# A memset on GpSimd behind the last accumulating DMA of a gated cross-attention and mixture-of-experts kernel

## The chip, the core and the metric

The kernel runs on one core of a Trainium2 chip. The metric is the device time of one launch in microseconds (us). The core has five engines that matter here, each with an instruction queue of its own: TensorE (PE in the profile, its weight loads PEld), VectorE (DVE), ScalarE (ACT), GpSimd (POOL) and SyncE (SP). They are held in order against each other by semaphores. Work that an engine's sequencer does itself (waits, branches, drains, issuing of DMAs) is written with a q: POOLq, SPq.

## The reference

The input `x` is 8 x 256 tokens of width 256. The reference adds a gated cross-attention to it and then a gated mixture of experts:

```python
x = x + tanh(g_xattn[0]) * xattn(layernorm(x), ctx, w_q, w_kv, w_out, b_out)   # 16 heads of 64, 120 context rows
x = x + tanh(g_ffn[0])   * ffn(layernorm(x), W1, W2, Wr)

def ffn(x, W1, W2, Wr):                       # 8 experts of width 1024, the best 2 of each token
    probs = softmax(x @ Wr.T)
    vals, idx = top_k(probs, 2)
    gate = one_hot(idx) weighted by vals / vals.sum()
    h = silu(x @ W1[e].T);  y = h @ W2[e].T   # for each expert e
    return sum over e of gate[e] * y
```

All of it is in float32.

## The kernel before, in words

The kernel first runs the attention, eight batches one after the other. While it does so it normalizes the attention's result, picks two experts for each token and scatters every token's row into a list in HBM (`routed`), one list for each expert. The attention's result itself is stored to the output `out`, so that the mixture of experts only has to be added to it.

In the second part the lists are worked off in tiles of 128 rows. The first eight tiles have a fixed expert, then come tiles of which a table computed on the chip says which rows and which expert they are (`order`, with `("full", j)` for j from 8 to 30). Tiles of four quarter lists (`quad`) run between them. For each tile, `up` multiplies by the first weight matrix, `down` multiplies by the second, scales by the gate into `y`, and `add_up` adds the 128 rows of `y` to the rows of `out` that they belong to. This is an indirect DMA issued from GpSimd with `compute_op=ALU.add`. As the same token stands in two lists, the adding DMAs must not overlap. The kernel therefore chains them by hand: each one waits until the one before it has landed, which the list `last_add` carries.

The order on TensorE, VectorE, ScalarE and SyncE is the order of the program text (`manual_schedule`); GpSimd is not in that list, but in the last part of the program it has nothing to run except the chained adding DMAs. The last `close_tile()` of the program issues the last `down` and with it the last adding DMA. Behind it the program ends: leaving the `TileContext` (line 1321 of the profile) emits, on every engine, the closing DRAIN and a barrier over all engines, with SP waiting for the outstanding DMAs first.

Of the kernel before, what the change touches and what calls it, by code (L numbers as in the profile page):

```python
# [9 lines left out]
F32 = mybir.dt.float32  # L10
# [5 lines left out]
P = 128  # L16
# [32 lines left out]
def tile_gated_xattn_moe(  # L49
# [978 lines left out]
    def close_tile():  # L1028
        if state["pending"] is not None:
            down(*state["pending"])  # L1030
            state["pending"] = None
# [248 lines left out]
            load_expert(7)  # L1280
    close_tile()


# [41 lines left out]
```

## Time and profile before

| what | us |
|---|---|
| median of 3 runs | 540.91 |
| lowest and highest run | 540.51, 541.64 |
| the profiled execution, device time | 540.71 |
| the profiled execution, span of its instructions | 538.9 |
| TensorE busy in it | 525.8 (98%) |
| VectorE, ScalarE, GpSimd busy | 285.1, 219.8, 128.7 |
| last TensorE work ends about | 528.6 |
| last adding DMA is issued at | 530.5 |

The span runs from the program's first instruction to its last. The 1.8 us between span and device time lie outside of the program's own instructions. The profile's page gives for each engine its busy time, then the span in slices, the DMA queues, the chain of work that ended last, and the costliest groups of instructions by source line. Instructions of a sequencer do not count as busy time, so a stretch in which only sequencers work looks empty in the slices; the views by source line show them.

### The profile page before, as it was taken

What the parts mean: (1) busy time and instruction counts of PE and PEld (TensorE: products, weight loads), DVE (VectorE), ACT (ScalarE), POOL (GpSimd) and SP (SyncE); (2) the same over time, 40 slices, a digit from 0 to 9 for tenths busy, and PEclk for the clock granted to TensorE, in tenths of its full rate; (3) what the DMA queues carried; (4) which work ended last, traced back from release to release, by engine and by line L of the source; (5) the groups of instructions that cost most, each with busy time, mean ns of one, the idle gap of its engine ahead of it and who ended that gap; (6) DMA issues with size and microseconds to landing.
All of it is one profiled execution on the core that took longest, in us unless ns stands there. A gap on an engine that the chain in (4) does not pass through costs nothing. (4 is left out here: it accounts for less than half of the span.)

```text
span 538.9 us, 9932 instructions
## 1 busy us (share of the span) xinstructions
PE 525.8 (98%) x3698; PEld 444.8 (83%) x3698; DVE 285.1 (53%) x683; ACT 219.8 (41%) x700; POOL 128.7 (24%) x135
## 2 busy tenths in 40 slices
PE   8999999999999999999999999999999999999992
PEld 7788887878878788787889999998997878889991
DVE  3675656567765677645663447444453453543530
ACT  1666546464664645557530311011144635501110
POOL 2011100000332003310014473222322124343422
PEclk9999999999999999999999999999999999999997
DMA  8999980140521401111099932312221210321311
GB/s 299 337 309 298 309 246 21 51 144 2 177 79 47 171 1 40 42 52 31 1 316 328 308 90 63 50 30 44 38 43 21 41 34 7 51 46 12 50 22 19
DMA packets 46439, 57.53 MB, mean 107 GB/s; under 512 B 3184, under 2 KB 41456, under 8 KB 46384
## 3 DMA queue, kind: packets, MB, share of 16 engines
q1 hardware_dynamic: 39488, 47.35, 28.6%
q0 software_dynamic: 6480, 8.81, 9.2%
q8 instruction: 32, 0.52, 0.4%
q10 hardware_dynamic: 416, 0.66, 0.4%
q14 instruction: 23, 0.19, 0.1%
HBM read 28.67 MB, written 28.27 MB: 106 GB/s over the span
## 5 line engine op out<-in xcount | busy, mean ns | idle before, releaser
L574 ACT ACTIVATE pr<-psc,mx 128x120 f32<-128x120 f32 x256 | 88.4, 372 | 64.5 <-DVE mx L568 64.5
L874 PEld LDWEIGHTS ph_full<-xT_full,w 128*128 128x128 f32 x736 | 85.0, 192 | 6.5 <-issue 5.7
L874 PE MATMUL ph_full<-xT_full,w 128*128 128x128 f32 x736 | 86.8, 276 | 0.3 <-PEq L1194 0.3
L890 PE MATMUL py_full<-w,hT_full 128*128 128x256 f32 x368 | 83.1, 379 | 0.0
L890 PEld LDWEIGHTS py_full<-w,hT_full 128*128 128x128 f32 x368 | 68.2, 190 | 8.4
L882 ACT ACTIVATE hT_full<-ph_full 128x1024 f32<-128x1024 f32 x23 | 23.5, 1023 | 97.7 <-PE ph_full L874 97.7
L524 PE MATMUL pq<-xnT,w_sb 128*128 128x256 f32 x256 | 62.7, 388 | 0.4 <-DVE xnT L207 0.4
L915 POOL DMA_INDIRECT out_dram<-y_full,xt_full x23 | 39.0, 1697 | 99.8 <-DVE y_full L898 70.4
L618 PE MATMUL pw<-w_sb 128*128 128x256 f32 x256 | 58.5, 382 | 0.0
L574 ACT ACTIVATION_READ_ACCUMULATOR pr<-psc,mx 128x1 f32 x256 | 55.7, 218 | 0.0
L524 PEld LDWEIGHTS pq<-xnT,w_sb 128*128 128x128 f32 x256 | 46.6, 190 | 10.8 <-issue 3.1
L618 PEld LDWEIGHTS pw<-w_sb 128*128 128x128 f32 x256 | 47.7, 190 | 9.0 <-issue 2.5
L562 DVE TENSOR_REDUCE mx<-psc 128x8 f32<-128x960 f32 x32 | 37.0, 1156 | 31.1 <-PE psc L554 31.1
L365 POOL DMA_INDIRECT routed<-rows,slot x32 | 32.1, 1002 | 54.4 <-DVE slot L361 47.4
L594 ACT COPY w_sb<-tr 120x512 f32<-120x512 f32 x64 | 34.6, 597 | 20.1 <-PE tr L593 20.1
L583 DVE TENSOR_TENSOR pr<-pr,sm 128x960 f32<-128x960 f32 x32 | 37.1, 1158 | 1.1
L554 PE MATMUL psc<-kT,w_sb 64*128 64x120 f32 x512 | 37.2, 284 | 0.0
L898 DVE TENSOR_SCALAR y_full<-py_full,gate 128x256 f32<-128x256 f32 x23 | 11.1, 484 | 48.5 <-PE py_full L890 44.8
L962 ACT COPY part<-w_sb 128x1024 f32 x32 | 31.1, 1043 | 14.1 <-PE py_q L1001 13.5
L554 PEld LDWEIGHTS psc<-kT,w_sb 64*128 64x128 f32 x512 | 31.1, 187 | 6.4 <-issue 3.6
L593 PEld LDWEIGHTS tr<-ident,pr 128*120 128x120 f32 x256 | 29.5, 138 | 5.5 <-issue 2.5
L845 DVE COPY w<-w_sb 128x2048 f32 x23 | 28.8, 1251 | 9.5 <-issue 4.3
(177 smaller groups left out, 670.6 us busy)
## 6 DMA issues: line engine op xcount, KB each, us to landing
routed<-w_sb SPq DMA_DIRECT2D x8, 2120.0 KB, 21.4
w_sb<-in_w1T_dram SPq DMA_DIRECT2D x8, 1024.0 KB, 5.7
w_sb<-in_w2T_dram SPq DMA_DIRECT2D x8, 1024.0 KB, 9.9
xt_full<-routed SPq DMA_DIRECT2D x23, 132.5 KB, 2.1
out_dram<-x SPq DMA_DIRECT2D x8, 256.0 KB, 2.4
x<-in_x_dram SPq DMA_DIRECT2D x7, 256.0 KB, 2.8
w_sb<-in_w_kv_dram SPq DMA_DIRECT2D x3, 512.0 KB, 8.0
xt_first<-routed SPq DMA_DIRECT2D x8, 132.5 KB, 2.5
```

What stands on the lines that cost most here:

```text
L365: send = nc.gpsimd.indirect_dma_start(out=routed[:, :], out_offset=bass.IndirectOffsetOnAxis(ap=slot[:, i : i + 1], axis=0), in_=rows[h][: ...
L524: nc.tensor.matmul(pq[:, i, :], lhsT=wq_sb[:, c, ts(2 * h + i, P)], rhs=xnT[:, c, :], start=(c == 0), stop=(c == DC - 1),)
L554: nc.tensor.matmul(psc[:, j, ts(i, M)], lhsT=qT[ts(j, DH), 4 * o + i, ts(nb, P)], rhs=kT[ts(j, DH), 4 * o + i, :], start=True, stop=True,)
L562: nc.vector.tensor_reduce(mx.rearrange("p (j i) -> p j i", i=4), psc[:, :, : 4 * M].rearrange("p j (i m) -> p j i m", m=M), AX.X, ALU.max,)
L574: nc.scalar.activation(pr[:, h, :], psc[:, j, ts(i, M)], AF.Exp, bias=mx[:, h : h + 1], scale=QK_SCALE, accum_out=sm[:, h : h + 1],)
L583: nc.vector.tensor_tensor(pr, pr, sm.unsqueeze(2).to_broadcast([P, 8, M]), ALU.mult)
L594: nc.scalar.copy(pT_sb[:, ts(j, 4), ts(nb, P)], tr[:M, :, :])
L618: nc.tensor.matmul(pw[:, :D], lhsT=oT_sb[b % 2][:, ci, ts(k, P)], rhs=wo_sb[:, ci, :], start=(ci == 0), stop=(ci == IC - 1),)
L874: nc.tensor.matmul(ph[:, f, :], lhsT=w1[:, c, ts(f, P)], rhs=xT[:, c, :], start=(c == 0), stop=(c == DC - 1),)
L890: nc.tensor.matmul(py[:, :D], lhsT=hT[:, f, :], rhs=w2[:, f, :], start=(f == 0), stop=(f == FC - 1),)
L915: add = nc.gpsimd.indirect_dma_start(out=out[:, :], out_offset=bass.IndirectOffsetOnAxis(ap=slots[:, k : k + 1], axis=0), in_=y[own, :], i ...
L962: nc.scalar.copy(w[:, q, :].rearrange("p (a b) -> p a b", b=D if down else DFF // 2), slab[:, ts(h, FC // 2), :] if down else slab[:, :, t ...
```

## The change

Behind the last `close_tile()` a tile of 128 x 1 float32 is allocated in the pool `const`, GpSimd sets it to zero, and that memset is given a dependency, with a semaphore wait, on the last adding DMA: it runs once the DMA has landed. Nothing reads the tile. No other line changes.

```diff
     close_tile()
 
+    end = const.tile([P, 1], F32, name="end")
+    mark = nc.gpsimd.memset(end, 0.0)
+    tc.add_manual_dep(
+        mark.ins,
+        last_add[-1].ins.name,
+        mybir.DependencyInfo(
+            mybir.DependencyClass.Sync, mybir.DependencyReason.DATA
+        ),
+        reason="behind the last sum",
+    )
+
```

## The prediction

> **What bounds the kernel now.** I read the page first, then the chain of waits that ended last, then the end of the span in windows, and last every instruction of the source line at which the program closes (L1321) and of the line that issues the sums (L915).
>
> ```profile
> span 538.9 us, 9932 instructions
> PE 525.8 (98%) x3698; PEld 444.8 (83%) x3698; DVE 285.1 (53%) x683; ACT 219.8 (41%) x700; POOL 128.7 (24%) x135
> ```
>
> Up to the last matmul TensorE is the bound: 525.8 of 538.9 us. The change does not touch any of that. It stands behind the last sum, so the question is only what fills the ten microseconds after TensorE.
>
> Windows of the end (columns: stretch, its length, busy time and count of PE, PEld, DVE, ACT, POOL, granted TensorE clock, DMA share, GB/s):
>
> ```profile
> 527.00:532.10 5.10, 1.61 (x8) 1.07 (x6) 0.48 (x1) 0.00 (x0) 2.05 (x2) 1.00 0.24 26
> 532.10:534.40 2.30, 0.00 (x0) 0.00 (x0) 0.00 (x0) 0.00 (x0) 0.00 (x0) 0.69 0.49 57
> 534.40:538.90 4.50, 0.00 (x0) 0.00 (x0) 0.00 (x0) 0.00 (x0) 0.00 (x0) 0.50 0.00 0
> ```
>
> The last sum's packets move in the middle window. In the third, 4.5 us long, no engine is busy and no DMA moves. What stands there is seen at the closing line (columns: engine, operation, count, shortest/median/longest in ns, first and last start in us):
>
> ```profile
> L1321 SPq EVENT_SEMAPHORE  x14: 17/28/4511, 512.8 to 538.9; - x14
> L1321 POOLq EVENT_SEMAPHORE  x4: 17/17/17, 538.1 to 538.8; - x4
> L1321 POOLq DRAIN  x3: 46/113/7812, 530.3 to 538.6; - x3
> L1321 DVEq DRAIN  x2: 19/272/524, 528.7 to 538.4; - x2
> ```
>
> GpSimd's first closing DRAIN takes 7812 ns. The chain of waits has its start, the timeline the last sum that it was dispatched with, and the waits of SP's queue what it costs SP:
>
> ```profile
> 530.27 1.77 POOLq L1321
> ...
> 530.49 1.54 POOL L915 DMA_INDIRECT out_dram<-y_full,xt_full  x1 [2.99 <-issue]
> ...
> DMA to landing us min/median/max: 2.2/3.8/8.1
> ...
> SPq L1321 <- PEq L1321: 3.9, 2, 3.4
> ```
>
> The DRAIN thus runs from 530.27 to 538.08. GpSimd's record of the last sum ends at 530.49 + 1.54 = 532.04. The sum lands at about 530.5 + 3.8 = 534.31 (SP's own record of its wait for that semaphore ends at 534.34). SP is through its list of waits at 534.87 and stands in the barrier for 3.4 us until GpSimd comes. So the end is set by GpSimd's DRAIN, and it lasts 6.04 us past the end of the sum's record and 3.77 us past its landing. After it, barrier and clearing of semaphores take 538.91 - 538.08 = 0.83 us.
>
> **The change part by part.** *The tile* is 4 bytes a partition that nobody reads; no address or order that the trace shows depends on it: nothing, if no other tile moves. *Removed or moved*: nothing. Every sum, load and matmul stays where it is, and nothing is queued behind the memset on GpSimd except the closing DRAIN; who waits for that DRAIN is the barrier, that is, all engines.
>
> *The wait.* The memset can begin when the last sum has landed, 534.31, plus the release: the wait ahead of the last sum ended 0.03 us after its semaphore's last step. That gives 534.34. It is 2.3 us after GpSimd's record was empty; in the kernel before those 2.3 us lay under the DRAIN, so by itself the wait costs nothing if the DRAIN needs the landing anyway, and 2.3 us if it does not.
>
> *The memset.* The nearest rows are the memsets of the same form at the program's start:
>
> ```profile
> L1306 POOL MEMSET const-float32-0.0<- x1: 99/99/99, 0.3 to 0.3; 128x1 f32 x1
> L1306 POOLq DRAIN  x1: 171/171/171, 0.4 to 0.4; - x1
> ```
>
> 0.10 us, so it ends at 534.44. Bound above: between the end of the wait at 529.78 and the last sum's dispatch GpSimd's sequencer spent 0.49 us; with that the memset would end at 534.93. I take 534.44, since a memset needs no DMA to be prepared.
>
> *The DRAIN behind it* is the whole question: the trace has no DRAIN of GpSimd that comes after a landed sum and a memset. The bounds from the nearest rows are 0.17 us (the DRAIN behind the four memsets at the start, no DMA issued before it) and 7.81 us (the long one whole). Between them lie 3.77 us (its part past the landing) and 6.04 us (its part past the sum's record). The tail after it stays 0.83 us. From the span of 538.91:
> - 0.17 us: ends at 534.61, but SP arrives only at 534.87, so the span would be 534.87 + 0.83 = 535.70, that is 3.2 us less;
> - 3.77 us: 534.44 + 3.77 + 0.83 = 539.04, 0.1 us more;
> - 6.04 us: 534.44 + 6.04 + 0.83 = 541.31, 2.4 us more;
> - 7.81 us: 543.08, 4.2 us more.
>
> I take 6.04 us. The long DRAIN isn't explained by waiting alone: when the data has landed, SP is released within 0.03 us, and still 3.77 us follow in which nothing moves. Something is being worked off, and the earliest it can have started is when GpSimd had handed out the last sum, at 532.04. The other engines' first closing DRAINs end with their last instruction (VectorE: 528.65 + 0.48 against 528.66 + 0.52), so the stretch belongs to GpSimd and to what it has done since the start: 73 indirect DMAs (32 + 23 + 8 + 8 + 2). The same engine's DRAIN before the first of these took 0.17 us and the one right after the long one 0.11 us, so the work is there once, after DMAs, and is gone when it has been done. Over 73 DMAs 6.04 us would be 0.08 us each. A memset after the landing does none of that work; it only starts it at 534.44 in place of 532.04.
>
> A rule of the Trainium skill speaks for the change: the page "PSUM — Partial Sum Buffer", section "Engine vs sequencer instructions", says that a drain waits until the engine is fully idle. By it alone the DRAIN would end with the memset and the sum would be the first line of the list above. The trace does not agree: the engine's last record ends at 532.04 and the DRAIN at 538.08.
>
> Another speaks against it: "GPSIMD Engine Reference", section "2.1 Instruction dispatch", has a cost of about 6 us, with no instruction of its own in the profile, for the first call to code just loaded. If the stretch of 6.04 us were such a load it would be paid behind the memset as well, and the sum would be the third line. No run here shows a loading of GpSimd's code.
>
> **The rivals.** *Short DRAIN, faster (0.36).* The long DRAIN may be long because it was dispatched with a DMA in flight: an inspection that found the sum unfinished and looked again only microseconds later. For it: the DRAIN does outlast the landing by a round 3.8 us without visible work, and with the landing waited for by a semaphore there is nothing unfinished to find. Against it: nothing else on this engine reacts that slowly; its waits for sums end 0.03 us after the landing. The price is the first line: 540.91 - 3.2 = 537.7. It decides when the DRAIN behind the memset takes less than 2.5 us.
>
> *Work that starts at the landing, no difference (0.14).* If the stretch of 3.77 us begins with the landing whatever stands between, the memset only shifts it by its own 0.13 us: 541.0. For it: 16 DMA engines looked at in turn at a quarter microsecond each would make such a stretch. Against it: VectorE and ScalarE show no such closing work, and nothing in the trace ties the 3.77 us to the landing rather than to the issue.
>
> *Fixed length, slower still (0.05).* If the DRAIN costs 7.81 us from its dispatch, the time is 545.1. Against it: 1.77 us of the 7.81 are the wait for the sum's record, which was under way.
>
> *The wait isn't there* could be the case if the memset were placed earlier or its wait were dropped; then it ends by 532.2 and the DRAIN is as before: 540.9 to 541.1, within the second rival's chance.
>
> **How the numbers follow.** The forecast, work of 6.04 us that starts behind the memset, has 0.42; 0.03 more is for shorter forms of it, 1.1 to 2 us over the time before. Its sum is made against the profiled execution: 540.71 + 2.40 = 543.11. That execution lies 0.20 us below the median of the runs, so a median would be 543.3. The runs lie from 0.40 below to 0.73 above their median, and the memset may be later by 0.49 us: the forecast's own range is 542.7 to 544.1. The whole range has to reach the fast rival: 537.7 less 0.4 gives 537.3. Above, it ends at 544.1 and leaves out the fixed length. A measurement of this kernel tells about 0.2% from no change, 1.08 us: slower by more has 0.42 + 0.03 + 0.05 = 0.50, within it 0.14, faster by more 0.36.
>
> **What would show it right or wrong.** In the profile of the changed kernel the closing line's first GpSimd DRAIN tells all: its start near 534.4 with a length near 6 us is the forecast, a length under 1 us the fast rival, near 3.8 us the neutral one. The memset should begin 0.03 to 0.5 us after the last landing and take 0.1 us. SP's wait in the barrier, 3.4 us before, should grow to near 5.7 us; under the fast rival it all but goes. If the span before 530.5 differs by more than a microsecond, the tile has moved something and the reasoning is wrong from its start.

## The result and the profile after

| | before | after |
|---|---|---|
| median of 6 runs, us | 540.70 | 543.42 |
| lowest and highest run, us | 540.42, 541.64 | 542.87, 544.57 |
| the profiled execution: device time, span, us | 540.71, 538.9 | 544.57, 542.8 |

The ratio after to before is 1.005, with a 95% interval from 1.004 to 1.0061: the memset makes the kernel 2.7 us slower by the medians and 2.45 us slower from lowest run to lowest run. The profiled execution of the changed kernel is the highest of its six, so it has to be read with care: not all of its 3.9 us are the change's.

First the page's head, then the end in windows cut at the same events as before (columns: stretch, its length, busy time and count of PE, PEld, DVE, ACT, POOL, granted TensorE clock, DMA share, GB/s):

```profile
span 542.8 us, 9933 instructions
```

```profile
528.40:533.50 5.10, 1.64 (x8) 1.11 (x6) 0.48 (x1) 0.00 (x0) 2.08 (x2) 0.94 0.24 26
533.50:535.80 2.30, 0.00 (x0) 0.00 (x0) 0.00 (x0) 0.00 (x0) 0.03 (x1) 0.50 0.50 57
535.80:542.77 6.97, 0.00 (x0) 0.00 (x0) 0.00 (x0) 0.00 (x0) 0.07 (x1) 0.50 0.00 0
```

One instruction more, the memset. The first two windows are as before. The third, in which no DMA moves and no engine but GpSimd is busy for 0.07 us, has grown from 4.50 to 6.97 us. The closing line, now L1332, says what stands there (engine, operation, count, shortest/median/longest in ns, first and last start), and the memset's own line what released it:

```profile
L1332 SPq EVENT_SEMAPHORE  x14: 17/28/4478, 512.8 to 542.7; - x14
L1332 POOLq EVENT_SEMAPHORE  x4: 17/17/17, 542.0 to 542.7; - x4
L1332 POOLq DRAIN  x3: 46/112/6179, 535.8 to 542.5; - x3
L1332 DVEq DRAIN  x2: 19/270/522, 530.1 to 542.2; - x2
```

```profile
L1284 POOL MEMSET end<- x1: 100/100/100, 535.8 to 535.8; 128x1 f32 x1
...
  DMA out_dram<-y_full,xt_full: 2.3, 1
```

GpSimd's first closing DRAIN has become shorter, 6179 ns in place of 7812, and it starts 5.5 us later. The timeline puts the four events in their order:

```profile
530.08 0.48 DVE L898 TENSOR_SCALAR y_full<-py_full,gate 128x256 f32<-128x256 f32 x1 [2.97 <-PE py_full L890]
531.93 1.55 POOL L915 DMA_INDIRECT out_dram<-y_full,xt_full  x1 [3.00 <-issue]
535.77 0.10 POOL L1284 MEMSET end<- 128x1 f32 x1 [2.29 <-DMA out_dram<-y_full,xt_full]
```

The last sum lands at 535.72, the memset runs from 535.77 to 535.87, and the DRAIN ends at 541.93, 6.06 us after the memset. SP, which stood 3.4 us in the barrier, stands there for 5.9:

```profile
SPq L1332 <- PEq L1332: 6.4, 2, 5.9
```

Part of the profiled execution's extra time arose 520 us earlier. The last `y` is made at 530.08 in place of 528.65, 1.43 us later. The timelines show where: the first matmuls of L480 wait for their weights in this execution and did not in the one before (first line after, second before).

```profile
8.75 2.04 PE L480 MATMUL pk<-ctxT_sb,w_sb 128*128 128x120 f32 x16 [1.36 <-DMA w_sb<-in_w_kv_dram]
```

```profile
7.34 1.96 PE L480 MATMUL pk<-ctxT_sb,w_sb 128*128 128x120 f32 x16
```

The tile isn't needed for it: of three kernels below that have the same tile and memset, two start these matmuls at 7.14 and 7.21, and the third, at 8.29, waits for the same load. It is a load at the program's start that lands now earlier, now later. The change's own cost is therefore read from the start of the last `y` to the end of the span: 538.91 - 528.65 = 10.27 us before, 542.77 - 530.08 = 12.70 us after, that is 2.43 us more.

### The profile page after: what moved, and what is told of

Same layout as the page of the kernel before. It is cut to its first block, busy times and chain, and to the rows that moved or that the text cites. A ratio compares the mean times of both kernels' runs of the same rounds, so it can differ in the third digit from the quotient of the medians.

```text
span 542.8 us, 9933 instructions
## 1 busy us (share of the span) xinstructions
PE 525.9 (97%) x3698; PEld 444.9 (82%) x3698; DVE 285.3 (53%) x683; ACT 219.8 (40%) x700; POOL 128.2 (24%) x136
## 5 line engine op out<-in xcount | busy, mean ns | idle before, releaser
L915 POOL DMA_INDIRECT out_dram<-y_full,xt_full x23 | 40.2, 1748 | 101.0 <-DVE y_full L898 75.0
```

The lines of the kernel that those rows point to most:

```text
L915: add = nc.gpsimd.indirect_dma_start(out=out[:, :], out_offset=bass.IndirectOffsetOnAxis(ap=slots[:, k : k + 1], axis=0), in_=y[own, :], i ...
```

## The experiments

The open question after the result was what GpSimd's DRAIN does for 6 us. The theory: it works off something for each DMA that GpSimd has issued since its last DRAIN, 0.083 us each. The rivals: a fixed stretch of 6 us, paid once or at each DRAIN; a stretch tied to the landing; the memset or its wait itself.

**The memset without its dependency.** The edit against the changed kernel:

```diff
-    mark = nc.gpsimd.memset(end, 0.0)
-    tc.add_manual_dep(mark.ins, last_add[-1].ins.name, ...)
+    nc.gpsimd.memset(end, 0.0)
```

> The memset stays at the end, its wait for the last landing is gone. Theory W (the closing DRAIN of GpSimd works off something left by the indirect DMAs, some 6.0 us, and starts it when GpSimd has nothing else to do): the memset runs right behind the last sum's record, about 0.2 us, and the DRAIN lies where it lay in the kernel before, over the landing: 540.7 to 540.9 us, 2.7 us less than with the wait, DRAIN ending about 6.1 us after the sum's record. Rival M (the memset itself, another kind of instruction between the DMAs and the DRAIN, is what costs): 543.4 us, as with the wait.

Measured: 540.64 us against 540.81, ratio 1.0004 (0.9995 to 1.0013). But the memset went elsewhere, as its row shows:

```profile
L1284 POOL MEMSET end<- x1: 89/89/89, 5.2 to 5.2; 128x1 f32 x1
```

With nothing to hold it, it was scheduled to 5.2 us after the program's start. The run shows that tile and instruction cost nothing; of a memset behind the last sum it tells nothing. It is repeated properly as the next one.

**The memset behind the last sum, without waiting for its landing.** The dependency is kept for the order in the queue alone:

```diff
-            mybir.DependencyClass.Sync, mybir.DependencyReason.DATA
+            mybir.DependencyClass.NoSync, mybir.DependencyReason.SCHED_ONLY
```

> The memset stands behind the last sum in GpSimd's queue, but without a wait for its landing (the memset of the earlier try without the wait had moved to the program's first microseconds, so that it told nothing of a memset behind the DMAs). Theory W (0.083 us of work for each DMA since the last DRAIN, begun when GpSimd is free): memset and DRAIN begin at the end of the last sum's record, the DRAIN ends 6.1 to 6.2 us after it, 540.7 to 541.0 us. Rival M (a memset between the DMAs and the DRAIN costs by itself): 543.4 us. If the DRAIN is long only because a DMA is in flight when it begins, it stays as before: 540.8 us.

Measured: 541.25 us against 540.84, ratio 1.0002 (0.9985 to 1.0018). Timeline of the end and closing DRAINs:

```profile
531.43 1.54 POOL L915 DMA_INDIRECT out_dram<-y_full,xt_full  x1 [2.99 <-issue]
532.41 0.68 POOL L1284 MEMSET end<- 128x1 f32 x1
```

```profile
L1332 POOLq DRAIN  x3: 46/113/7912, 531.2 to 539.7; - x3
```

The memset's record starts before the sum's has ended (532.98) and ends 0.11 us after it, at 533.09. The DRAIN ends at 539.15, 6.06 us behind the memset, though the sum only lands at 535.17. From the last `y` to the end of the span there are 10.39 us, 0.12 more than before, about as much as the memset's end lies behind the sum's record. So neither the memset nor its place in the queue costs anything that the times of the runs show; the wait does, because it holds back the start of a stretch of 6.06 us which, with 73 DMAs, begins just as well while the sum is in flight.

**One DRAIN in an idle stretch in the middle.** The edit against the kernel before, in `add_up`, so that GpSimd drains while it waits for the next tile anyway:

```diff
             last_add.append(add)
+            if t == ("full", 15):
+                settled = nc.gpsimd.drain()
+                tc.add_manual_dep(settled.ins, add.ins.name, ...Sync, DATA...)
```

> The kernel before with one DRAIN of GpSimd more, behind the landing of the sum of full tile 15, at about 410 us; 50 of the 73 indirect DMAs come before it and 23 after it. GpSimd is idle there for 6 us. Theory W, with 6.04 / 73 = 0.083 us for each DMA since the last DRAIN: the new DRAIN takes 4.1 us, the closing one has 1.9 us of work and ends with the landing of the last sum, at about 534.4 in the clock of the profile before, so 3.2 us less: 537.5 us. Rival F (6 us once, whatever came before, such as the loading of code): the new DRAIN takes 6 us, the closing one none, 537.5 us as well, but the length of the new one tells them apart. Rival G (every DRAIN behind DMAs takes 6 us): 6 us at both places, 540.7 us or a little more. Rival L (a DRAIN needs 3.8 us from the last landing): the new one 3.8 us, the closing one unchanged, 540.7 us.

Measured: 537.82 us against 540.81, ratio 0.9946 (0.9932 to 0.996). The added DRAIN's line, the closing DRAINs and SP's wait in the barrier:

```profile
L939 POOLq DRAIN  x1: 4157/4157/4157, 409.5 to 409.5; - x1
```

```profile
L1331 POOLq DRAIN  x3: 46/112/4923, 529.9 to 535.4; - x3
```

```profile
SPq L1331 <- PEq L1331: 1.2, 2, 0.6
```

Behind 50 DMAs, all landed, the added DRAIN takes 4.16 us (4.1 expected), and the closing one ends 4.9 us after its start instead of 7.8. A stretch that is paid once would have gone to the added DRAIN whole; a fixed one at each DRAIN would show 6 us twice. Neither does. One thing missed: with 23 DMAs left, work of 1.9 us that starts at the sum's record (531.68) would have been over before the landing at 533.86, and the DRAIN ended at 534.84, 0.98 us behind it.

**That DRAIN and the memset of the change.** Here everything has landed when the closing DRAIN starts its work.

> The changed kernel (memset behind the landing) with one DRAIN more behind the landing of the sum of full tile 15, so that 23 DMAs are left for the closing DRAIN. Theory W: the closing DRAIN begins behind the memset, 0.13 us after the landing, and takes 23 x 0.083 = 1.9 us; the end is 2.9 us after the landing (1.9 + 0.13 + 0.83), where it was 6.06 + 0.13 + 0.83 = 7.0 us in the changed kernel: 539.3 us, 4.1 us less than the changed kernel and 1.0 to 1.5 us more than with the additional DRAIN alone (537.8). If the DRAIN's work were the same whatever is left: 543.4 us.

Measured: 539.15 us against 540.84, ratio 0.9966 (0.9955 to 0.9977).

```profile
534.52 0.10 POOL L1294 MEMSET end<- 128x1 f32 x1 [2.31 <-DMA out_dram<-y_full,xt_full]
```

```profile
L1342 POOLq DRAIN  x3: 46/113/2069, 534.5 to 537.1; - x3
```

The DRAIN ends at 536.575, 1.954 us behind the memset's end at 534.621. With 73 DMAs the same stretch behind the same memset takes 6.06 us; with 23 it takes 1.95. The memset's wait, its place and its landing are the same in both: the stretch goes by the DMAs.

**Two DRAINs, the second three tiles before the end** (behind `("full", 15)` and `("full", 28)`).

```diff
-            if t == ("full", 15):
+            if t in (("full", 15), ("full", 28)):
```

> The kernel before with two DRAINs of GpSimd more: behind the landing of the sum of full tile 15 and behind that of full tile 28, where 2.2 us lie before the next sum; 2 DMAs are left for the closing DRAIN. Theory W: the second DRAIN takes 21 x 0.083 = 1.75 us and delays nothing, the closing DRAIN ends about 0.1 us after the last landing; then SP's list of waits, 0.55 us after the landing, is last: about 0.4 us less than with one additional DRAIN, 537.4 us, which is the floor of this way. If the 0.98 us by which the closing DRAIN outlasted the landing there are a fixed cost: 537.8 us.

Measured: 537.79 us against 540.84, ratio 0.994 (0.9923 to 0.9957).

```profile
L939 POOLq DRAIN  x2: 1757/2957/4157, 410.3 to 524.0; - x2
```

```profile
L1331 POOLq DRAIN  x3: 46/113/4121, 531.0 to 536.0; - x3
L1331 SPq DRAIN  x3: 7/7/13, 535.4 to 535.7; - x3
```

The first again takes 4157 ns; the second, behind 21 more DMAs, 1757. Two are left for the closing one; it ends at 535.08, 0.12 us behind the landing (534.96), and now SP is last: it reaches its own DRAIN only at 535.4. So the second DRAIN gains little: from the last `y` to the span's end there are 7.08 us against 7.36 with one, and the medians, 537.79 and 537.82, don't tell the two kernels apart. The time expected, 537.4, was 0.4 us too low.

**A DRAIN early** (behind `("full", 9)`, 42 DMAs after the start, 31 left), to settle what happens while the last sum is in flight.

```diff
-            if t == ("full", 15):
+            if t == ("full", 9):
```

> The additional DRAIN of GpSimd stands behind the landing of the sum of full tile 9, at about 365 us: 42 DMAs before it, 31 left for the closing one. Theory W: the new DRAIN takes 42 x 0.083 + 0.02 = 3.5 us. With 23 left the closing DRAIN had ended 0.98 us after the landing, though 1.9 us of work from the end of the record would have been over before it. If half of the work has to wait for the landing of the sum in flight: with 31 left it ends 0.083 x 31 / 2 = 1.3 us after it. If it is a fixed delay: 0.98 us. If the work is done in one go from the record: 2.6 us after the record, 0.3 us after the landing. Time in all three 537.5 to 538.3 us.

Measured: 538.30 us against 540.79, a single run of each, so only the trace is read here.

```profile
L939 POOLq DRAIN  x1: 3500/3500/3500, 365.5 to 365.5; - x1
```

```profile
L1331 POOLq DRAIN  x3: 52/113/5245, 530.5 to 536.3; - x3
```

The added DRAIN takes the 3.5 us expected. The closing one ends at 535.74, 1.31 us behind the landing at 534.43. The stretch behind the landing is thus neither a constant (0.98) nor gone (0.1 to 0.3): with 2, 23 and 31 DMAs left it is 0.12, 0.98 and 1.31 us, in each case close to half of 0.083 us times the number.

**More DMAs: four kernels.** Each adds 32 DMAs from GpSimd that write a constant to a scratch tensor that nobody reads. Large ones have 128 rows of 512 bytes, small ones 16 rows of 128 bytes.

```diff
+    aside = tc.dram_tile([32 * P, P], F32, name="aside")
...
+        if b == 5 and k == 2:
+            for m in range(32):
+                nc.gpsimd.dma_start(aside[ds(m * P, 128), :128], ones[:128, :128])
```

The first two (large, and small with `16` and `:32`) had nothing to hold them in the middle.

> The kernel before with 32 more DMAs issued from GpSimd in the idle time of the sixth batch of the attention (from about 250 us on), each of 128 rows of 512 bytes from a constant tile into a scratch tensor that nobody reads. Theory W with 0.083 us for each DMA: the closing DRAIN has 105 DMAs to work off, 8.7 us from the end of the last sum's record: 2.65 us more than before, 543.4 us. Rivals F, G and L (a fixed length): 540.7 us, as long as the additional DMAs delay nothing.

> As with 32 more DMAs of 128 rows, but each of 16 rows of 128 bytes. If the work of the closing DRAIN is by the DMA: 543.4 us, as with the large ones. If it is by the row or the descriptor: an eighth of it, 0.3 us more than before, 541.0 us. Fixed length: 540.7 us.

Measured: 550.26 us (large) and 551.15 us (small) against 540.81, ratios 1.016 (1.014 to 1.018) and 1.0193 (1.0173 to 1.0213). Most of that isn't the DRAIN. The DMAs were scheduled to the program's start, among the first loads. Windows of the first 40 us, kernel before and kernel with the small ones:

```profile
0.00:40.00 40.00, 37.60 (x259) 31.27 (x260) 22.59 (x70) 19.88 (x80) 5.65 (x22) 1.00 1.02 315
```

```profile
0.00:40.00 40.00, 31.80 (x200) 26.16 (x202) 16.35 (x60) 15.63 (x61) 20.46 (x53) 0.91 1.02 303
```

TensorE does 200 matmuls there in place of 259. The times are no measure of the DRAIN, but its own length is:

```profile
L1326 POOLq DRAIN  x3: 46/113/8349, 540.8 to 549.7; - x3
```

```profile
L1326 POOLq DRAIN  x3: 46/112/10426, 537.9 to 548.9; - x3
```

With the small ones (second fence) it ends 8.66 us behind the last sum's record: 105 DMAs at 0.0825 us. With the large ones it ends only 6.58 us behind it, where 8.7 were expected.

The other two hold the 32 DMAs back to about 238 us, where the loads are through:

```diff
+        if b == 6 and k == 3:
+            for m in range(32):
+                extra = nc.gpsimd.dma_start(aside[ds(m * P, 16), :32], ones[:16, :32])
+                tc.add_manual_dep(extra.ins, sends[-1].ins.name, ...Sync, DATA...)
```

> The kernel before with 32 more small DMAs of GpSimd (16 rows of 128 bytes each), now held back until the first scatters of the second group of batches have landed, at about 235 us, since in the earlier try they had moved to the program's start and delayed its loads by some 8 us. Theory W: the closing DRAIN ends 105 x 0.083 = 8.7 us after the last sum's record, 2.6 us more than before: 543.4 us, if nothing on the way waits for the additional DMAs. Fixed length: 540.8 us.

> As with the 32 small DMAs held back to about 235 us, but each of 128 rows of 512 bytes. At the program's start such large ones had lengthened the closing DRAIN by only 0.5 us, where the small ones had lengthened it by 2.6. Theory W alone (0.083 us for each DMA since the last DRAIN): the closing DRAIN ends 8.7 us after the last sum's record. Theory W with a bound (what is left by DMAs has room for a limited number of rows, and the oldest is worked off when it is full): 6.0 to 7.0 us, whenever the large ones are issued. If at the start it was the place and not the size: 8.7 us.

Measured: small 543.90 us against 540.84, ratio 1.0056 (1.0034 to 1.0078); large 541.39 us against 540.79, a single run of each. The last sum and the closing DRAINs, small, then large:

```profile
531.03 1.54 POOL L917 DMA_INDIRECT out_dram<-y_full,xt_full  x1 [3.05 <-issue]
```

```profile
L1334 POOLq DRAIN  x3: 46/113/10426, 530.8 to 541.8; - x3
```

```profile
530.57 1.54 POOL L917 DMA_INDIRECT out_dram<-y_full,xt_full  x1 [2.94 <-issue]
```

```profile
L1334 POOLq DRAIN  x3: 46/113/8426, 530.4 to 539.3; - x3
```

The small ones, at a place where they delay nothing, add 2.6 us to the stretch, which ends 8.66 us behind the sum's record, and 3.06 us to the kernel's median (from the last `y` to the end of the span: 2.68 us). So a DMA of 16 short rows costs as much as one of the sums. The large ones add less: the DRAIN ends 6.66 us behind the record, and 6.58 where they came early. From the landing, though, the two agree to the nanosecond: the last sum lands at 534.433 and the DRAIN ends at 538.777, and with the early ones at 544.817 and 549.161, in both 4.344 us later. Half of 0.083 us times 105 is 4.36. Read this way, the half of the stretch that comes behind the landing is there in full, and only the half ahead of it is shorter: it is over by the landing, 2.2 to 2.3 us behind the record, where half of the 8.66 us would take 4.3. This is a reading of two traces; no DRAIN behind large DMAs was run that starts with everything landed. The 6.0 to 7.0 us expected of a bound on what is left for the DRAIN were met, but no run shows such a bound, and why the first half is shorter stays open.

## Why the prediction was right

Put together, the DRAINs that started with everything landed:

| DMAs since the last DRAIN | length, us | 0.083 x number + 0.02 |
|---|---|---|
| 21 (second of the two added) | 1.757 | 1.76 |
| 23 (added one and memset, closing) | 1.954 | 1.93 |
| 42 (added behind tile 9) | 3.500 | 3.51 |
| 50 (added behind tile 15) | 4.157 | 4.17 |
| 73 (the changed kernel, closing) | 6.061 | 6.08 |

The slope is (6.061 - 1.757) / 52 = 0.083 us for each DMA.

*The tile, nothing:* held; without its dependency the same memset changes nothing that can be measured.

*The memset, 0.03 to 0.5 us behind the landing and 0.10 us long:* it came 0.05 us behind it and took 0.10 us.

*The DRAIN behind it, 6.04 us, as work of 73 DMAs at 0.08 us each:* 6.06 us, and the number of DMAs as its cause is shown by taking them away (23, 21) and adding small ones (105). The time since the last DRAIN, which an added DRAIN shortens as well, isn't the cause: the 32 small DMAs lengthen the stretch from 6.04 to 8.66 us at the same distance from it. The reason given for choosing 6.04 us, that the stretch can have started no earlier than the sum's record, agrees with the memset without a wait: the same 6.06 us, but from 533.09.

*The sum, +2.40 us:* the part of the trace that the change touches grew by 2.43 us. The medians differ by 2.72, the lowest runs by 2.45.

*SP's wait, near 5.7 us:* 5.9.

*"If the span before 530.5 differs by more than a microsecond, the tile has moved something":* it differs by 1.43 us, and the conclusion drawn there was wrong. The shift comes from the wait for `w_kv` at 7.4 us. That test should have been written on the stretch from the last `y` to the end, since a single execution's start varies by more than the test allowed.

*The short DRAIN, the chief rival at 0.36,* is ruled out by the same row: no DMA was in flight when the DRAIN began, and it still took 6 us. Its price was right for a DRAIN that is short: with two added DRAINs there are 7.08 us from the last `y` to the end in place of 10.27, the 3.2 us less that the prediction gave for it. The Trainium skill's page "PSUM — Partial Sum Buffer", section "Engine vs sequencer instructions", has a drain wait until the engine is fully idle. The traces show that this isn't all on GpSimd: engine idle from 535.87, all DMAs landed, and the DRAIN ends at 541.93.

*The load of code, which would have given the same number:* "GPSIMD Engine Reference", section "2.1 Instruction dispatch", has about 6 us for the first call to code just loaded. That the trace showed 6 us as well was chance; DRAINs of 1.76, 3.50 and 4.16 us, two of them in one program, don't fit a load of fixed length.

*The fixed length from the dispatch (0.05)* would have shown 7.81 us again; the DRAIN's record is 6.18.

*The stretch tied to the landing (0.14)* has a true part that the prediction missed. With the 73 DMAs of the kernel before, the work is bound by its length from the sum's record, 6.04 us. With few left, the landing sets the end, plus about half of the work: 0.12, 0.98 and 1.31 us with 2, 23 and 31 DMAs, and 4.344 with 105 of which 32 are large, in each case 0.041 us for each DMA and some 0.04 us more. Read together: without the large DMAs, the DRAIN ends at the later of the two, the record's end plus 0.083 us per DMA, or the landing plus half of that. For the kernel before the second is 534.31 + 3.0 = 537.3, the first 538.1, and 538.08 was measured. With the large ones the second alone fits.

What the DRAIN does for each DMA, and why about half of it comes behind the last landing, no run here shows.

## What to carry to other kernels

When a program ends some microseconds after its last data has landed, look at the closing line by engine: a sequencer's DRAIN isn't counted as busy, and the windows show it only as emptiness. Here a DRAIN of GpSimd that begins with everything landed costs 0.083 us for every DMA that the engine issued since its last one, so where that work outlasts the landing, anything that makes it start later, even a memset of 0.1 us with a wait, moves the end by the whole delay. The opposite move pays: one DRAIN where GpSimd waits anyway made the kernel before 3 us faster (537.82 us, ratio 0.9946), and it is enough that most of the DMAs lie before it: a second one just ahead of the end brought 0.28 us more in the trace and nothing that the medians show.

## What the runs showed of the hardware that was not expected

- The 0.083 us per DMA are the same for 16 rows of 128 bytes and for the 128-row sums, but 32 additional DMAs of 128 rows x 512 bytes lengthen the stretch by only 0.5 to 0.6 us where 32 small ones add 2.6. By the reading above what they leave out lies ahead of the last landing: behind it there are 4.344 us, half of 0.083 us for each of 105 DMAs.
- Another instruction of GpSimd's sequencer grows with the DMAs as well. At the start of the table's loop it takes 1040 ns in the kernel before, with 43 DMAs issued by then, 1696 with 32 more, the same for large and small, and 205 where a DRAIN stood one DMA before it:

```profile
L1194 POOLq INC_SWDGE_SEM  x1: 1040/1040/1040, 373.2 to 373.2; - x1
```

```profile
L1207 POOLq INC_SWDGE_SEM  x1: 1696/1696/1696, 373.7 to 373.7; - x1
```

```profile
L1204 POOLq INC_SWDGE_SEM  x1: 205/205/205, 373.9 to 373.9; - x1
```

- A memset that is dispatched behind a DMA still being issued has a record of 0.68 us in place of 0.10, but ends 0.11 us after that DMA's record.
